# Half tiles of the output projection between the last three value products of attention, and its inputs by groups in a fixed order

## The chip, the cores and the metric

The kernel runs on one core of a Trainium2 chip. The core has five engines with a queue each: TensorE (PE, matrix products), VectorE (DVE), ScalarE (ACT), GpSimd (POOL), and SyncE (SP), which here issues the transfers (DMAs). The time of a run is the device time in microseconds. The kernel before takes 3853.54 us, the median of 3 runs (3845.11 to 3853.94). The profile is of one further execution, which took 3845.32 us, with a span of 3843.2 us from its first to its last instruction.

## The reference

The input x has shape 2 x 48 x 48 x 768 in fp32: two images (batches), 2304 tokens each, 768 channels. Two layers follow each other, each added to its input:

```python
x = x + _L0_conv_ref(_gn(x), qkv_w, qkv_b, proj_w, proj_b, rel_pos_h, rel_pos_w)
x = x + _L1_conv_ref(_gn(x), w1, b1, w2, b2)
```

`_gn` is a group norm over 32 groups of 24 channels. Layer 0 is attention with 12 heads of 64 channels over all 2304 tokens, with a relative position bias by row and by column, and an output projection:

```python
attn = einsum('bqc,bkc->bqk', q * scale, k) + rel_h[..., :, None] + rel_w[..., None, :]
out = softmax(attn) @ v          # heads put side by side
return out @ proj_w + proj_b
```

Layer 1 takes a two-dimensional Fourier transform of the image, applies two small complex matrix layers with a GELU between them to 8 blocks of 96 channels, shrinks small values to zero, and transforms back.

## The kernel before

Each batch goes through attention, the projection and the spectral layer, one after the other.

**Attention** works on two heads (a pair, six of them) and 128 queries at a time. This is a unit; there are 108 of them, numbered n = 0 to 107, and the loop of `attention` runs to n = 110, since a unit's work is spread over three iterations. In iteration n:

- `scores(n)`: TensorE multiplies queries by keys (ps_s), and VectorE adds the bias tile s in place and keeps the maximum.
- `numerators(n)`: ScalarE takes the exponential of s.
- `weigh(n - 2)`: TensorE multiplies the turned numerators pT of the unit two before by the values v (ps_o). This is the value product. The code weighs unit n - 2 at iteration n, so units 105, 106 and 107 have their value products at n = 107, 108 and 109, the last two without scores beside them.
- `squares` and `exchange` of unit n - 1, second half, and of unit n, first half: VectorE turns 32 x 32 squares, and each half goes into pT by 6 transfers from SyncE and 2 copies on ScalarE. The first half of unit n waits until the value product of unit n - 2 has read the buffer that it takes, since there are two pT buffers.
- `finish(n - 2)`: ScalarE copies ps_o out, and after every third unit SyncE stores a piece of the attention output to oT in memory.
- `new_unit(n + 1)` (line 340): GpSimd makes the next bias tile s from rhw. There are three s buffers, so it waits for the exchange of unit n - 2.
- `inverses`: after each half of a pair, the inverses of the softmax sums are turned (ps_i), copied and stored to inv_d.
- At n = 102 to 108 the loop calls `late()`, which makes one step of the projection's preparation.

The names pe, dve, act and sync in `attention` are `InOrder` objects: every instruction that they issue is pinned behind whatever was written before it for the same engine. Line 67 is the helper's, so most of attention's instructions are recorded on it. Instructions called on `nc` directly are not pinned in front, and a scheduler with a cost model places them before the build is finished; a pinned instruction written later still stays behind them.

**Projection.** `Projection` takes over the memory of the normed input, once no unit reads it any more. It holds the weights w (two transfers, lines 585 and 586), a bias row for all partitions, pb, and two buffers for groups of attention output. `tokens(g)` loads group g (384 tokens, three tiles of 128) from oT (line 631) and the inverses from inv_d (line 633, two transfers into one buffer), and GpSimd scales the group (line 637). The seven steps before are: weights, weights, nothing, `tokens(0)`, nothing, the bias row, `values_bias`. The last works for batch 0 only: the value bias goes through the weights (24 matmul instructions, ps_pb, line 612), VectorE adds both halves to pb (line 619), and the row is kept in memory (pb_d, line 621) for batch 1, which loads it with line 600.

`project_out` then loads the rows of x (x2, six groups of 4 x 96 tokens, line 653), and GpSimd adds pb to each of the four (line 655). All six groups' loads are written ahead of the loop. For each tile t of 18 and each half of the channels (a half tile, 384 columns), TensorE accumulates acc from six pairs of instructions (line 691) in a PSUM bank, and VectorE adds it to the rows (line 700), by pieces of 32 to 96 rows. The pool ps_b has 7 PSUM banks. When two more rows of x2 are complete, `over_w` makes the first Fourier transform of them (ps_y, line 671, 8 instructions), ScalarE copies it (line 678), and SyncE stores it to y_d (line 679). When a row is complete, `tile_stats` computes its group sums: VectorE reduces (line 724) and scales (line 725), GpSimd subtracts (line 727), ScalarE squares (line 730), VectorE reduces (line 731). None of the instructions of `project_out` is pinned.

**Spectral** takes the rest; its transfers of weights (line 844) may be placed among the projection's.

Of the kernel before, what the change touches and what calls it, by code (L numbers as in the profile page):

```python
# [9 lines left out]
F32 = mybir.dt.float32  # L10
# [6 lines left out]
P = 128  # L17
# [140 lines left out]


def attention(tc, k, x_b, a, oT, inv_d, late, span, ps_b, ps_o):  # L160

# [10 lines left out]
    with ExitStack() as ctx:  # L172
# [319 lines left out]
        for n in range(len(order) + 3):  # L492
            un = older = None
            if n < len(order):
                un = ahead
                pr, g, x = order[n]
                if g == 4 and x == 0 and pr + 1 < NP:
                    weights[0] = load_w(0, pr + 1)
                scores(un)
                recent.append(un)  # L500
            write = read = None
            if un is not None:
                numerators(un)
                ready, staged = staged, None
                if x == 2:
                    if n + 4 < len(order):
                        key = order[n + 4][:2]
                        staged = (key, queries(*key))
                    if g == 2 and pr + 1 < NP:
                        weights[2] = load_w(2, pr + 1)  # L510
                    if g == 5 and pr + 2 < NP:
                        weights[1] = load_w(1, pr + 2)
                elif n < 2:
                    for i in range(3):
                        values(0, 3 * n + i)
                    if n:
                        weights[1] = load_w(1, 1)
                elif pr + 1 < NP:
                    i = 2 * g + x
                    for j in range(0 if n == 3 else i, i + 1):  # L520
                        (keys if j < 6 else values)(pr + 1, j % 6)
                if ready is not None:
                    key, qT = ready
                    rhw, write, read = relative(key[1], qT)
                    groups[key] = (qT, rhw)
            if turn is not None:
                turn()
                turn = None
            if n > 1 and recent:
                older = recent.pop(0)  # L530
                weigh(older)
            evict(by_act)
            if last is not None:
                squares(last, 1)
                exchange(last, 1)
            if write is not None:
                write()
            if un is not None:
                squares(un, 0)
# [30 lines left out]
class Projection:  # L570


    def __init__(self, tc, k, a, oT, inv_d, span, ps_b, dram):
        self.nc = nc = tc.nc
        self.k, self.a, self.ps_b, self.dram = k, a, ps_b, dram
        self.oT_v = oT.rearrange("(cc p) s -> p cc s", p=P)
        self.inv_d = inv_d
        self.whole = span.tile([P, NCC * S], F32, tag="span", name="proj")
        self.w = self.whole[:, : NCC * C].rearrange("p (cc f) -> p cc f", f=C)
        self.pb = self.whole[:, NCC * C : (NCC + 1) * C]  # L580
        self.o = {}
        w_v = a["proj_w"].rearrange("(cc p) f -> p cc f", p=P)
        half = NCC // 2
        self.steps = [
            lambda: nc.sync.dma_start(out=self.w[:, :half], in_=w_v[:, :half]),
            lambda: nc.sync.dma_start(out=self.w[:, half:], in_=w_v[:, half:]),
            lambda: None,
            lambda: self.tokens(0),
            lambda: None,
            self.bias,  # L590
            self.values_bias,
        ]

    def step(self):
        self.steps.pop(0)()

    def bias(self):

        src = self.a["proj_b"] if self.k.pb_d is None else self.k.pb_d
        self.nc.sync.dma_start(out=self.pb, in_=src.partition_broadcast(P))  # L600

    def values_bias(self):


        nc, k = self.nc, self.k
        if k.pb_d is not None:
            return
        for hf in range(2):
            cols = slice(hf * UQ, (hf + 1) * UQ)
            ps = self.ps_b.tile([P, 512], F32, tag="b", name="ps_pb")  # L610
            for cc in range(NCC):
                nc.tensor.matmul(
                    ps[:, :UQ],
                    lhsT=k.bv[:, cc : cc + 1].to_broadcast([P, P]),
                    rhs=self.w[:, cc, cols],
                    start=(cc == 0),
                    stop=(cc == NCC - 1),
                )
            nc.vector.tensor_tensor(self.pb[:, cols], ps[:, :UQ], self.pb[:, cols], ALU.add)
        k.pb_d = self.dram.tile([C], F32, tag="pb_d", name="pb_d")  # L620
        nc.sync.dma_start(out=k.pb_d, in_=self.pb[0, :])

    def tokens(self, g):

        nc = self.nc
# [5 lines left out]
        nc.sync.dma_start(out=o_sb, in_=self.oT_v[:, :, g * UQ : (g + 1) * UQ])  # L631
        for h in range(2):
            nc.sync.dma_start(
                out=inv[h * HD : (h + 1) * HD],
                in_=self.inv_d[:, g // 3, h, g % 3, :].partition_broadcast(HD),
            )
        nc.gpsimd.tensor_tensor(o_sb, o_sb, inv, ALU.mult)  # L637
        self.o[g] = o_sb


def project_out(tc, k, x_b, pr, pools, y_d, x2, stats, constants):

# [18 lines left out]
    dev = small.tile([R, HW // 2, NG], F32, tag="dev", name="dev")  # L661
# [1 line left out]
    def over_w(g):  # L663

        y1 = work.tile([YP, 2, C], F32, tag="y1", name="y1")
        part = x2[2 * g // XP]
        t0 = 2 * g % XP
        for s in range(C // SC):
            ch = slice(s * SC, (s + 1) * SC)
            ps = bank("ps_y")  # L670
            nc.tensor.matmul(
                ps[:YP, : 2 * SC],
                lhsT=k.fw,
                rhs=part[:, t0 : t0 + 2, ch],
                start=True,
                stop=True,
            )
            nc.scalar.copy(y1[:, :, ch], ps[:YP, : 2 * SC].rearrange("p (t c) -> p t c", c=SC))
        nc.sync.dma_start(out=y_d[:, 2 * g : 2 * g + 2, :], in_=y1)

    done = turned = 0
    for t in range(NT):
        if t % 3 == 0:
            if t // 3 not in pr.o:
                pr.tokens(t // 3)
            o_sb = pr.o[t // 3]
        for hf in range(2):
            cols = slice(hf * UQ, (hf + 1) * UQ)
            acc = bank("acc")
            for cc in range(NCC):  # L690
                nc.tensor.matmul(  # L691
                    acc[:, :UQ],
                    lhsT=o_sb[:, cc, (t % 3) * P : (t % 3 + 1) * P],
                    rhs=pr.w[:, cc, cols],
                    start=(cc == 0),
                    stop=(cc == NCC - 1),
                )
            for p, hp, q, n in shifts(t):
                dst = row(hp)[q : q + n, cols]
                nc.vector.tensor_tensor(dst, acc[p : p + n, :UQ], dst, ALU.add)  # L700
# [62 lines left out]
class Spectral:  # L763
# [50 lines left out]
    def bank(self, name):  # L814
        return self.ps_b.tile([P, 512], F32, tag="b", name=name)
# [211 lines left out]
def block_kernel(tc, a, out):  # L1027
    nc = tc.nc
    B = a["x"].shape[0]
    with ExitStack() as ctx:  # L1030
# [20 lines left out]
        for b in range(B):  # L1051
# [6 lines left out]
            def late():  # L1058
                if not ready:
                    ready.append(Projection(tc, k, a, oT, inv_d, span, ps_b, dram))  # L1060
                ready[0].step()

            attention(tc, k, a["x"][b], a, oT, inv_d, late, span, ps_b, ps_o)
            with ExitStack() as ctx2:
# [115 lines left out]
```

## Time and profile before

| what | value |
|---|---|
| median of 3 runs | 3853.54 us (3845.11 to 3853.94) |
| the profiled execution | 3845.32 us, span 3843.2 us |
| busy: PE / PEld / DVE / ACT / POOL | 95% / 68% / 77% / 65% / 54% |
| chain that ended last, by engine | PE 81%, DMA 6%, DVE 5%, POOL 4%, SP's queue 2% |
| batch 0: end of the last value product, end of the projection's last ps_y | 1472.97 us, 1661.35 us |
| batch 1: the same | 3388.3 us, 3580.5 us |
| DMA share, 1385 to 1405 / 1425 to 1445 / 1495 to 1505 us | 0.98 / 1.02 / 1.04 |

The timeline of an engine has, on each line, the start and the duration in us, the engine, the line of the code, the operation, output<-inputs, the memory shapes and the number of instructions merged; in brackets stands the idle time of the engine ahead of it and who ended it. PE's instructions in fp32 go in pairs, so a half tile is 12 of them. A table by stretches has for each stretch its length, the engine's busy time, the granted clock of TensorE as a share of full speed, the mean busy share of the 16 DMA engines and GB/s.

### The profile page before, as it was taken

What the parts mean: (1) busy time and instruction counts of PE and PEld (TensorE: products, weight loads), DVE (VectorE), ACT (ScalarE), POOL (GpSimd) and SP (SyncE); (2) the same over time, 40 slices, a digit from 0 to 9 for tenths busy, and PEclk for the clock granted to TensorE, in tenths of its full rate; (3) what the DMA queues carried; (4) which work ended last, traced back from release to release, by engine and by line L of the source; (5) the groups of instructions that cost most, each with busy time, mean ns of one, the idle gap of its engine ahead of it and who ended that gap; (6) DMA issues with size and microseconds to landing.
All of it is one profiled execution on the core that took longest, in us unless ns stands there. A gap on an engine that the chain in (4) does not pass through costs nothing.

```text
span 3843.2 us, 83225 instructions
## 1 busy us (share of the span) xinstructions
PE 3661.7 (95%) x31464; PEld 2599.0 (68%) x31464; DVE 2950.0 (77%) x6642; ACT 2502.4 (65%) x3549; POOL 2063.9 (54%) x646
## 2 busy tenths in 40 slices
PE   8999999999999988989989999999999999779898
PEld 6677776767777655567566777777677776555675
DVE  4788888888889885654457988889888899846544
ACT  3688888888888882222137888888888888812221
POOL 2466666666666666321125666666666666663111
PEclk9999999999999999999989999999999999889899
DMA  3677777777777888434526777777777777884344
GB/s 100 143 174 169 173 171 167 175 165 178 167 171 171 172 195 199 126 90 119 165 83 138 172 174 169 174 167 174 168 174 168 173 170 168 202 195 114 90 119 133
DMA packets 496092, 606.92 MB, mean 158 GB/s; under 512 B 180109, under 2 KB 310797, under 8 KB 495694
## 3 DMA queue, kind: packets, MB, share of 16 engines
q1 hardware_dynamic: 495694, 601.61, 67.2%
q8 instruction: 250, 4.10, 0.5%
q14 instruction: 148, 1.21, 0.1%
HBM read 131.53 MB, written 87.67 MB: 57 GB/s over the span
## 4 chain that ended last, share of the span: by engine, by line
PE 81%; DMA 6%; DVE 5%; POOL 4%; SPq 2%; issue 1%; ACT 1%; POOLq 0%; DVEq 0%; ACTq 0%
PE ps_o L67 20%; PE ps_s L67 19%; PE ps_proj L67 14%; PE ps_v L67 8%; PE acc L691 5%; DVE s L67 4%; PE ps L926 4%; POOL s L340 3%; DMA pT<-s 2%; SPq L67 2%; PE ps_z L874 2%; PE ps_u L957 2%; PE ps_x L981 2%; PE ps L899 2%; PE ps L903 2%; PE ps_r L67 1%
## 5 line engine op out<-in xcount | busy, mean ns | idle before, releaser
L340 POOL TENSOR_TENSOR s<-rhw 128x2304 f32<-128x2304 f32 x432 | 1744.8, 4060 | 1152.1 <-DMA pT<-s 552.7
L67 DVE CUSTOM_DVE_ANT_0 s<-ps_s,s 128x512 f32<-128x512 f32 (+1 forms) x2160 | 1223.5, 633 | 372.9 <-issue 247.9
L67 ACT ACTIVATE s<-s,nm 128x1152 f32<-128x1152 f32 x864 | 1074.7, 1245 | 448.3 <-DVE nm L67 409.4
L67 DVE STREAM_TRANSPOSE s<-s 128x1152 f32<-128x1152 f32 x864 | 1111.8, 1344 | 5.5 <-ACT s L67 5.5
L67 ACT COPY pT<-s 32x1152 f32<-32x1152 f32 x864 | 993.3, 1150 | 24.5 <-PE ps_o L67 9.1
L67 PE MATMUL ps_o<-pT,v 128*64 128x128 f32 x15552 | 923.8, 279 | 70.8 <-DMA pT<-s 49.7
L67 PEld LDWEIGHTS ps_o<-pT,v 128*64 128x64 f32 x15552 | 872.0, 140 | 134.1 <-issue 66.1
L67 PE MATMUL ps_s<-kT,qT 64*128 64x512 f32 (+1 forms) x4320 | 918.2, 559 | 13.5 <-DVE mx L67 10.1
L67 PEld LDWEIGHTS ps_s<-kT,qT 64*128 64x128 f32 x4320 | 431.5, 187 | 449.7 <-issue 334.2
L67 PE MATMUL ps_proj<-xnT,w 128*128 128x384 f32 (+1 forms) x2016 | 600.2, 452 | 3.7 <-ACT gn_rstd L148 3.7
L67 PEld LDWEIGHTS ps_proj<-xnT,w 128*128 128x128 f32 x2016 | 362.4, 192 | 211.9 <-DVE mx L67 41.0
L691 PE MATMUL acc<-proj 128*128 128x384 f32 x864 | 292.0, 498 | 25.5 <-POOL proj L637 14.9
L67 PEld LDWEIGHTS ps_v<-w,xnT 128*128 128x128 f32 x2592 | 295.5, 193 | 21.5 <-DVE mx L67 21.5
L67 PE MATMUL ps_v<-w,xnT 128*128 128x128 f32 x2592 | 307.7, 279 | 0.0
L943 POOL TENSOR_TENSOR spectrum<-spectrum 128x480 f32<-128x480 f32 x80 | 96.3, 1204 | 325.8 <-DVE spectrum L942 322.1
L691 PEld LDWEIGHTS acc<-proj 128*128 128x128 f32 x864 | 168.4, 196 | 145.6 <-issue 20.4
L730 ACT ACTIVATE st_xc<-st_xc 96x768 f32<-96x768 f32 x48 | 40.5, 843 | 234.6 <-POOL st_xc L727 234.6
L67 DVE DVE_READ_ACCUMULATOR2_ANT mx<- 128x1 f32 x2160 | 179.4, 83 | 0.0
L700 DVE TENSOR_TENSOR x<-acc,x 32x384 f32<-32x384 f32 (+2 forms) x216 | 119.6, 553 | 77.6 <-PE acc L691 73.5
L67 ACT ACTIVATION_READ_ACCUMULATOR s<-s,nm 128x1 f32 x864 | 161.2, 187 | 0.0
L907 ACT ACTIVATE spectrum<-ps,b 96x400 f32<-96x400 f32 x96 | 56.5, 589 | 140.1 <-PE ps L903 140.1
L727 POOL TENSOR_TENSOR st_xc<-x,local 96x768 f32<-96x768 f32 x48 | 70.9, 1481 | 142.9 <-DVE local L725 120.9
(96 smaller groups left out, 2217.8 us busy)
## 6 DMA issues: line engine op xcount, KB each, us to landing
pT<-s SPq DMA_DIRECT2D x2592, 144.0 KB
t<-rel SPq DMA_DIRECT2D x144, 189.0 KB
rhw<-t SPq DMA_DIRECT2D x144, 144.0 KB
y_d<-y SPq DMA_DIRECT2D x24, 672.0 KB
y<-y_d SPq DMA_DIRECT2D x40, 360.0 KB
u_d<-spectrum SPq DMA_DIRECT2D x40, 360.0 KB
u<-u_d SPq DMA_DIRECT2D x48, 300.0 KB
xt<-in_x SPq DMA_DIRECT2D x12, 1152.0 KB
```

The lines of the kernel that those rows point to most:

```text
L67: return lambda *args, **kw: self.tc.keep_in_program_order(op(*args, **kw))
L340: nc.gpsimd.tensor_tensor(s[:, h, :].rearrange("p (y x) -> p y x", x=HW), rhw[:, x, h, :HW][:, :, None].to_broadcast([P, HW, HW]), rhw[:, ...
L691: nc.tensor.matmul(acc[:, :UQ], lhsT=o_sb[:, cc, (t % 3) * P : (t % 3 + 1) * P], rhs=pr.w[:, cc, cols], start=(cc == 0), stop=(cc == NCC - 1),
L700: nc.vector.tensor_tensor(dst, acc[p : p + n, :UQ], dst, ALU.add)
L727: nc.gpsimd.tensor_tensor(xc, x3, local[:, :, None].to_broadcast([xt.shape[0], NG, GC]), ALU.subtract)
L874: nc.tensor.matmul(ps[:BS, w * 96 : (w + 1) * 96], lhsT=self.y2[s, j][:, w, i * BS : (i + 1) * BS], rhs=k.fh, start=True, stop=True,)
L899: nc.tensor.matmul(ps[:BS, :400], lhsT=w1[:, wa, i, :], rhs=zf[:, 0, fs], start=True, stop=False,)
L903: nc.tensor.matmul(ps[:BS, :400], lhsT=w1[:, wb, i, :], rhs=zf[:, 1, fs], start=False, stop=True,)
L926: nc.tensor.matmul(ps[64 * r : 64 * r + 64, w * BS : (w + 1) * BS], lhsT=self.o1[:, ri, f0 : f0 + 64], rhs=w2[:, (0, 2, 1, 0)[2 * r + ri], ...
L943: nc.gpsimd.tensor_tensor(val, val, clip, ALU.subtract)
L957: nc.tensor.matmul(ps[: 2 * HW, :480], lhsT=k.ih, rhs=d2[:, c0 : c0 + 480], start=True, stop=True)
L981: nc.tensor.matmul(ps[: 2 * HW, : 2 * SC], lhsT=k.iw, rhs=self.u2[s, i][:, t : t + 2, :], start=True, stop=True,)
```

## The change

1. *Filling.* `Projection` gets a list `waiting`: for batch 0 the two halves of `values_bias`, then the half tiles of tiles 0 to 2; for batch 1 the half tiles alone. The attention loop takes from it ahead of the last three value products: one at n = 107, two at n = 108, two at n = 109. Batch 0 so makes both bias halves and three half tiles there, batch 1 five half tiles. A new function `product(t, hf)` makes a half tile's accumulation and keeps its bank until `project_out` adds it to the rows.
2. *Steps.* The seven steps become: weights, weights, `tokens(0)`, the bias row, nothing, nothing, `tokens(1)`. So group 0 is loaded at n = 104 instead of 105, the bias row at n = 105 instead of 107, and group 1 at n = 108, where it came with `project_out` before.
3. *Groups one ahead.* `project_out` loads two groups of rows ahead of the loop (the constants between them). At tiles 3, 6, 9 and 12 it loads the next group of attention output and then the next group of rows.
4. *Fixed order.* The matmuls of the half tiles, the bias and `over_w`, the loads of groups and rows, the stores to y_d, and the scaling and row additions on GpSimd go through `InOrder` objects.

```diff
+            if n >= len(order) - 1 and recent:
+                late(1 if n < len(order) else 2)
             if n > 1 and recent:
                 older = recent.pop(0)
                 weigh(older)
...
+        self.pe, self.sync, self.pool = (
+            InOrder(tc, e) for e in (nc.tensor, nc.sync, nc.gpsimd)
+        )
         self.steps = [
             lambda: nc.sync.dma_start(out=self.w[:, :half], in_=w_v[:, :half]),
             lambda: nc.sync.dma_start(out=self.w[:, half:], in_=w_v[:, half:]),
+            lambda: self.tokens(0),
+            self.bias,
             lambda: None,
-            lambda: self.tokens(0),
             lambda: None,
-            self.bias,
-            self.values_bias,
+            lambda: self.tokens(1),
         ]
+        self.accs, self.waiting = {}, []
+        if k.pb_d is None:
+            self.waiting += [lambda hf=hf: self.values_bias(hf) for hf in range(2)]
+        for t in range(3):
+            self.waiting += [lambda t=t, hf=hf: self.product(t, hf) for hf in range(2)]
...
+    def fill(self, n):
+
+        for _ in range(n):
+            self.waiting.pop(0)()
...
+    def product(self, t, hf):
+
+        if (t, hf) not in self.accs:
+            o_sb = self.o[t // 3]
+            acc = self.ps_b.tile([P, 512], F32, tag="b", name="acc")
             for cc in range(NCC):
-                nc.tensor.matmul(
+                self.pe.matmul(
+                    acc[:, :UQ],
+                    lhsT=o_sb[:, cc, (t % 3) * P : (t % 3 + 1) * P],
+                    rhs=self.w[:, cc, hf * UQ : (hf + 1) * UQ],
                     start=(cc == 0),
                     stop=(cc == NCC - 1),
                 )
+            self.accs[t, hf] = acc
+        return self.accs[t, hf]
...
-    for i, part in enumerate(x2):
-        nc.sync.dma_start(out=part, in_=x_v[:, i * XP : (i + 1) * XP, :])
+
+    def rows(i):
+
+        part = x2[i]
+        pr.sync.dma_start(out=part, in_=x_v[:, i * XP : (i + 1) * XP, :])
         for j in range(XP):
-            nc.gpsimd.tensor_tensor(part[:, j, :], part[:, j, :], pr.pb[:R], ALU.add)
-        if i == 0:
-            constants()
-            pr.tokens(1)
+            pr.pool.tensor_tensor(part[:, j, :], part[:, j, :], pr.pb[:R], ALU.add)
+
+    rows(0)
+    constants()
+    rows(1)
...
     for t in range(NT):
-        if t % 3 == 0:
-            if t // 3 not in pr.o:
-                pr.tokens(t // 3)
-            o_sb = pr.o[t // 3]
+        if t % 3 == 0 and 0 < t < NT - 3:
+            pr.tokens(t // 3 + 1)
+            rows(t // 3 + 1)
         for hf in range(2):
             cols = slice(hf * UQ, (hf + 1) * UQ)
-            acc = bank("acc")
...
+            acc = pr.product(t, hf)
```

More of the change, by code (lines that the diff above doesn't have):

```diff
@@ L600, in bias, with values_bias @@
         self.nc.sync.dma_start(out=self.pb, in_=src.partition_broadcast(P))
-    def values_bias(self):
+    def values_bias(self, hf):
         nc, k = self.nc, self.k
[L606 to L610, printed above, removed]
+        cols = slice(hf * UQ, (hf + 1) * UQ)
+        ps = self.ps_b.tile([P, 512], F32, tag="b", name="ps_pb")
+        for cc in range(NCC):
+            self.pe.matmul(
+                ps[:, :UQ],
+                lhsT=k.bv[:, cc : cc + 1].to_broadcast([P, P]),
+                rhs=self.w[:, cc, cols],
+                start=(cc == 0),
+                stop=(cc == NCC - 1),
+            )
+        nc.vector.tensor_tensor(self.pb[:, cols], ps[:, :UQ], self.pb[:, cols], ALU.add)
+        if hf:
+            k.pb_d = self.dram.tile([C], F32, tag="pb_d", name="pb_d")
+            nc.sync.dma_start(out=k.pb_d, in_=self.pb[0, :])
+    def product(self, t, hf):
+        if (t, hf) not in self.accs:
+            o_sb = self.o[t // 3]
+            acc = self.ps_b.tile([P, 512], F32, tag="b", name="acc")
             for cc in range(NCC):
[L612 to L615, printed above, removed]
+                self.pe.matmul(
+                    acc[:, :UQ],
+                    lhsT=o_sb[:, cc, (t % 3) * P : (t % 3 + 1) * P],
+                    rhs=self.w[:, cc, hf * UQ : (hf + 1) * UQ],
                     start=(cc == 0),
@@ L618, in values_bias @@
                 )
-            nc.vector.tensor_tensor(self.pb[:, cols], ps[:, :UQ], self.pb[:, cols], ALU.add)
-        k.pb_d = self.dram.tile([C], F32, tag="pb_d", name="pb_d")
-        nc.sync.dma_start(out=k.pb_d, in_=self.pb[0, :])
+            self.accs[t, hf] = acc
+        return self.accs[t, hf]
     def tokens(self, g):
-        nc = self.nc
         at = [(NCC + 1) * C + i * NCC * UQ for i in range(3)]
@@ L630, in tokens @@
         )
-        nc.sync.dma_start(out=o_sb, in_=self.oT_v[:, :, g * UQ : (g + 1) * UQ])
+        self.sync.dma_start(out=o_sb, in_=self.oT_v[:, :, g * UQ : (g + 1) * UQ])
         for h in range(2):
-            nc.sync.dma_start(
+            self.sync.dma_start(
                 out=inv[h * HD : (h + 1) * HD],
@@ L636, in tokens @@
             )
-        nc.gpsimd.tensor_tensor(o_sb, o_sb, inv, ALU.mult)
+        self.pool.tensor_tensor(o_sb, o_sb, inv, ALU.mult)
         self.o[g] = o_sb
@@ L670, in over_w @@
             ps = bank("ps_y")
-            nc.tensor.matmul(
+            pr.pe.matmul(
                 ps[:YP, : 2 * SC],
@@ L678, in over_w @@
             nc.scalar.copy(y1[:, :, ch], ps[:YP, : 2 * SC].rearrange("p (t c) -> p t c", c=SC))
-        nc.sync.dma_start(out=y_d[:, 2 * g : 2 * g + 2, :], in_=y1)
+        pr.sync.dma_start(out=y_d[:, 2 * g : 2 * g + 2, :], in_=y1)
     done = turned = 0
     for t in range(NT):
-        if t % 3 == 0:
-            if t // 3 not in pr.o:
-                pr.tokens(t // 3)
-            o_sb = pr.o[t // 3]
+        if t % 3 == 0 and 0 < t < NT - 3:
+            pr.tokens(t // 3 + 1)
+            rows(t // 3 + 1)
         for hf in range(2):
             cols = slice(hf * UQ, (hf + 1) * UQ)
-            acc = bank("acc")
[L690 to L697, printed above, removed]
+            acc = pr.product(t, hf)
             for p, hp, q, n in shifts(t):
@@ L1056, in block_kernel, with late @@
             ready = []
-            def late():
+            def late(fill=0):
                 if not ready:
                     ready.append(Projection(tc, k, a, oT, inv_d, span, ps_b, dram))
-                ready[0].step()
+                if fill:
+                    ready[0].fill(fill)
+                else:
+                    ready[0].step()
             attention(tc, k, a["x"][b], a, oT, inv_d, late, span, ps_b, ps_o)
```

## The prediction

> **What bounds the kernel now.** I read the page first, then the TensorE timeline around the end of attention in each batch, then the same stretch for GpSimd, SyncE and VectorE, and last the table by stretches. On the page TensorE is busy 95% of the span and holds 81% of the chain that ended last; what a change can win is TensorE's idle time and half-clock time. TensorE, end of batch 0's attention and start of its projection (start, us, operation, in brackets the idle time before it and who ended it):
>
> ```profile
> 1439.83 1.92 PE L67 MATMUL ps_s<-kT,qT 64*128 64x512 f32 x6 [0.60 <-DVE mx L67]
> 1441.68 8.01 PE L612 MATMUL ps_pb<-proj,bv 128*128 128x384 f32 x24
> 1450.15 4.15 PE L67 MATMUL ps_o<-pT,v 128*64 128x128 f32 x72 [0.47 <-ACT s L67]
> 1458.54 6.71 PE L67 MATMUL ps_o<-pT,v 128*64 128x128 f32 x72 [4.23 <-DMA pT<-s]
> 1468.82 4.15 PE L67 MATMUL ps_o<-pT,v 128*64 128x128 f32 x72 [3.57 <-DMA pT<-s]
> 1473.02 31.13 PE L691 MATMUL acc<-proj 128*128 128x384 f32 x96
> ...
> 1529.60 7.04 PE L691 MATMUL acc<-proj 128*128 128x384 f32 x12 [8.68 <-DVE x L700]
> 1541.57 10.06 PE L691 MATMUL acc<-proj 128*128 128x384 f32 x24 [4.93 <-POOL proj L637]
> ```
>
> The last scores end at 1441.75, the three last value products (ps_o, units 105 to 107) stand apart, and the projection itself stops twice. Batch 1 has the same shape without ps_pb:
>
> ```profile
> 3362.53 7.03 PE L67 MATMUL ps_o<-pT,v 128*64 128x128 f32 x72 [6.34 <-DMA pT<-s]
> 3372.24 5.62 PE L67 MATMUL ps_o<-pT,v 128*64 128x128 f32 x72 [2.68 <-DMA pT<-s]
> 3382.84 5.45 PE L67 MATMUL ps_o<-pT,v 128*64 128x128 f32 x72 [4.98 <-DMA pT<-s]
> ...
> 3459.00 10.49 PE L691 MATMUL acc<-proj 128*128 128x384 f32 x24 [9.97 <-POOL proj L637]
> ```
>
> GpSimd: the bias tile of unit 107 (L340) and the scaling of group 0 (L637), of each batch:
>
> ```profile
> 1430.43 8.08 POOL L340 TENSOR_TENSOR s<-rhw 128x2304 f32<-128x2304 f32 x2 [1.66 <-DMA pT<-s]
> 1447.40 5.13 POOL L637 TENSOR_TENSOR proj<-proj 128x2304 f32<-128x2304 f32 x1 [8.89 <-DMA proj<-inv_d]
> ...
> 3344.72 8.07 POOL L340 TENSOR_TENSOR s<-rhw 128x2304 f32<-128x2304 f32 x2 [2.02 <-ACT res L67]
> 3358.26 5.09 POOL L637 TENSOR_TENSOR proj<-proj 128x2304 f32<-128x2304 f32 x1 [5.46 <-DMA proj<-inv_d]
> ```
>
> SyncE's queue, where group 0's loads stand behind the exchange of unit 105's first half:
>
> ```profile
> 1408.09 23.53 SPq L67 DMA_DIRECT2D pT<-s  x24
> 1431.67 0.59 SPq L631 DMA_DIRECT2D proj<-oT  x1
> 1432.30 1.49 SPq L633 DMA_DIRECT2D proj<-inv_d  x2
> ```
>
> VectorE, two L725 during runs of GpSimd row additions: one got in after 1.26 us, one only after 10.22:
>
> ```profile
> 1502.48 1.26 DVE L725 TENSOR_SCALAR local<-local 96x32 f32<-96x32 f32 x1
> 1514.04 10.22 DVE L725 TENSOR_SCALAR local<-local 96x32 f32<-96x32 f32 x1
> ```
>
> The stretches from the end of the last value product to the projection's last matmul, both batches (length, PE busy, clock, DMA share, GB/s):
>
> ```profile
> 1472.97:1661.35 188.38, 174.76 (x526) 0.95 0.54 138
> 3388.30:3580.50 192.20, 176.90 (x529) 0.96 0.52 134
> ```
>
> Pure work there: 36 half tiles of 3.87 us (31.13 is eight) = 139.3, and 12 transforms of 2.58 = 31.0, together 170.3. So 18.1 and 21.9 us are idle or at half clock.
>
> **What the Trainium skill says.** "SBUF — State Buffer", Who interferes with whom: a VectorE tensor_scalar in a 2-port mode and a GpSimd instruction take one shared port pair as an exclusive lock, and the second blocks. The trace agrees (10.22 us against 0.18 undisturbed). "TensorE: Matmul & The Clock Gate", What's actually happening: about 3.4 us of idling halves the clock until as long a busy window. It agrees: 12 matmuls took 7.04 us after 8.68 idle. Same page, Architectural detail: VectorE, ScalarE and GpSimd are strict FIFO, so a waiting instruction holds all behind it. GpSimd's lines agree.
>
> **The change, part by part.**
>
> *Filling.* 3 half tiles (batch 0, with both bias halves, which stood there before) and 5 (batch 1) leave the stretch after the last value product: 3 x 3.87 = 11.6 and 5 x 3.87 = 19.4 us. Left after it: 33 half tiles + transforms = 127.7 + 31.0 = 158.7, and 31: 120.0 + 31.0 = 151.0.
>
> *Group 0's loads one iteration earlier* (n = 104, not 105). Three transfers issue in 2.0 us in SyncE's idle stretch from 1419.9, ahead of the second-half exchange of unit 104 (1423.86). By the semaphore records transfers land nearly in issue order: the exchange's pieces every 0.75 us, and group 0's three took 12.7 us (1434.5 to 1447.2) in batch 0, 9.5 in batch 1. Before, they delayed unit 105's second half only, and no bias tile came after it. Now they delay unit 104's, which frees the buffer that unit 107's bias tile needs. Batch 0: queue free at 1424.1, group 0 landed at 1436.8, exchange at 1439.3. GpSimd scales group 0 first (5.1 us, to 1441.9), then L340 runs 1441.9 to 1450.0 instead of 1430.4 to 1438.5. Scores end at 1452.6, against 1441.75. Batch 1: landed 3347.5, scaled to 3352.6, L340 to 3360.7 (before 3352.8), scores end 3363.3, against 3356.2.
>
> *TensorE's fixed order from there*, gapless. Batch 0: 2 x 4.0 (bias) + 3 x 3.87 + 3 x 4.15 = 32.1, so the last value product ends at 1484.7, **11.7 later** than 1472.97. Batch 1: 5 x 3.87 + 12.45 = 31.8, 3395.1, **6.8 later** than 3388.3. Does the data come? Batch 0's exchanges: VectorE's bias addition (0.55, now ahead of the transposes of L67) ends at 1457.3, the transposes at 1459.8 and 1462.4, SyncE issues 6 pieces in 3.85; unit 107's second half waits for the second bias addition (1465.3), lands near 1474.5, needed at 1480.5. Covered by 6 us; were that gone, it would be lost one for one. The waits added here: on VectorE the two bias additions wait for TensorE, and behind the second stand unit 107's last transposes (before at 1449.96), then their exchange, then the last value product. On TensorE each value product now waits behind half tiles, and its copy to SBUF and the inverses behind it: that is the 11.7 and 6.8. The 0.64 us bias issue moves two iterations up, into a lull: nothing.
>
> *Row loads after the inverses.* Before, row group 0 was issued at 1465.94 and landed at 1473.51, 7.6 later. Now it stands in SyncE's order behind the inverses' three stores: the last value product, 0.8 for the copy, 2.4 for the stores, 7.6: 10.8 us after that product. Two row additions (2 x 1.77) and VectorE (0.6) free the first PSUM bank at 15.0. There are 7. Batch 0 holds 3 and fills 4 more until 15.6: no wait. Batch 1 holds 5, fills two by 7.8 and waits 7.2. Then the first transform (after the fourth tile, in fixed order) needs tiles 0 and 1 added: row statistics and six more additions, at 21.5. TensorE gets there at 19.5 and 18.9: waits 2.0 and 2.6. L725 is the unknown: it may slip in at the next instruction's end (counted) or be held to the end of eight row additions, 25.2, 7 us more. Nothing excludes either; of six L725 in such runs four slipped in. I take half, 3.5 a batch, and 1.5 for the clock at half speed.
>
> *Groups one ahead.* From tile 3 on, a group's TensorE time is 6 x 3.87 + 2 x 2.58 = 28.4. Loads issued at its start land after 11.5, are scaled by 16.6, rows added by 23.7 (four of 1.77): hidden with 11.8 and 4.7 to spare. GpSimd needs 5.1 + 7.1 + 4 x 1.48 = 18 of 28.4. The stops of 8.68, 4.93 and 9.97 go; they are in the 188.4 and 192.2. If that cover goes, each hand-over costs what it is late. Stores of y_d in fixed order wait for work already done: nothing.
>
> **Sum.** Batch 0: 188.4 - 11.7 - 158.7 - 2.0 - 5.0 = 11.0. Batch 1: 192.2 - 6.8 - 151.0 - 9.8 - 5.0 = 19.6. Together 30.6, say 30, off the profiled execution's 3845.3 (span 3843.2): 3815. Of the three runs shown one lies with it and two 8 us above, which makes the median 3853.5; I take the middle, **3819**.
>
> **Rivals.**
> *A, bias tile not delayed*: the small exchange pieces pass the big loads, L340 starts on time. For: transfers overlap in part. Against: unit 105's pieces issued at 1436.6 landed at 1447.9. It gives back up to 11.7 and 6.8: 49 off, about 3801.
> *B, scaling queued ahead of unit 106's bias tile too*: GpSimd then waits for group 0's landing with two bias tiles behind it. L340 of 106 starts at 1441.9 instead of 1420.7, unit 107's scores end 8 to 9 us later still, twice 9. With L725 held in both batches (7): about 5 off, 3844. For: the scaling is pinned in front. Against: unit 106's tile is not pinned and is ready first.
> *C, slower*: every group hand-over late. GpSimd scales and adds strictly in order, so a load that lands late holds row additions and statistics, and fixed-order TensorE stops. Eight hand-overs (four a batch); 30 / 8 = 3.8 us each decides, that is loads landing near 27 us instead of 11.5. At 6 each: 48 - 30, 18 slower, 3863 to 3872. For: at the start the queue is full (a row group waited 30 us in it). Against: that was five row groups at once; now one.
>
> **How the numbers follow.** Likeliest 0.55, A 0.15, B 0.17, C 0.13. Likeliest alone: 3805 to 3835 (L725 both ways, either run level). Range: 3792 (A with both L725 free) to 3852 (B with the upper level). Three runs spread by 0.23%, so 0.3% (11.6 us) is about what can be told from no change: all of the likeliest and A, a little of B are faster, 0.73; most of B same, 0.14; C slower, 0.13.
>
> **What would show it.** Right: no ps_o with idle before it at the end of attention; L340 of unit 107 some 8 to 11 us later against its predecessors; L725 and a bank wait near 8 to 30 us after the last ps_o; no idle at L637 afterwards. Wrong: unit 107's tile on time (A), a POOL wait on proj<-inv_d before unit 106's tile (B), TensorE waiting on POOL or DVE at every third tile (C), or value products that still wait for pT.

## The result, and the profile after

The changed kernel takes **3835.99 us** (median, 3832.68 to 3840.88), beside 3852.39 us of the kernel before in the same comparison (3845.11 to 3855.07): a ratio of **0.9964**, 95% interval 0.9952 to 0.9976. It is 16.4 us faster; 3819 and about 30 us (34.5 between the prediction's 3819 and the median of before that it used, 3853.5) had been forecast. Two later comparisons gave 0.9965 and 0.9971. The direction was right, and about half of the gain is there.

First the page of the profiled execution of the changed kernel: its span, and TensorE's row (busy time, share of the span, instructions).

```profile
span 3834.6 us, 83183 instructions
PE 3656.9 (95%) x31464; PEld 2586.8 (67%) x31464; DVE 2940.0 (77%) x6642; ACT 2496.3 (65%) x3549; POOL 2063.2 (54%) x646
```

The span is 8.6 us shorter than before's 3843.2. The forecast for this pair was 30.6, so 22 us have to be found. (The profiled execution of before took 3845.32 us, well under its kernel's median of 3852.39, which is why this pair shows less than the medians.)

TensorE's timeline at the end of batch 0's attention, to be held against the first view of the prediction:

```profile
1451.15 4.14 PE L67 MATMUL ps_pb<-proj,bv 128*128 128x384 f32 x12
1455.22 4.15 PE L67 MATMUL ps_o<-pT,v 128*64 128x128 f32 x72
1459.30 4.14 PE L67 MATMUL ps_pb<-proj,bv 128*128 128x384 f32 x12
...
1471.32 8.01 PE L67 MATMUL acc<-proj 128*128 128x384 f32 x24
1479.26 4.15 PE L67 MATMUL ps_o<-pT,v 128*64 128x128 f32 x72
```

No value product waits any more, and the last one ends at 1483.4. GpSimd's timeline shows why the scores end 9.5 us later: the bias tile of unit 107 (L341 now) comes after the scaling of group 0, which had waited for its load.

```profile
1436.03 5.07 POOL L67 TENSOR_TENSOR proj<-proj 128x2304 f32<-128x2304 f32 x1 [8.02 <-DMA proj<-inv_d]
1441.06 8.07 POOL L341 TENSOR_TENSOR s<-rhw 128x2304 f32<-128x2304 f32 x2
```

Both went as worked out (1441.9 for the bias tile, 1484.7 for the last value product). Now the table by stretches, from the end of the last value product to the last transform, both batches (length, then busy time and instructions of PE, PEld, DVE, ACT and POOL, granted clock, DMA share, GB/s):

```profile
1483.41:1660.28 176.87, 165.22 (x493) 91.73 (x493) 116.84 (x179) 37.20 (x71) 102.17 (x57) 0.98 0.57 145
3393.45:3568.68 175.23, 160.53 (x469) 89.48 (x469) 115.56 (x176) 37.74 (x71) 99.69 (x56) 0.95 0.58 146
```

Of 158.7 and 151.0 us of pure TensorE work they are 18.2 and 24.2 us too long; 7.0 and 14.8 had been forecast. (In the kernel before, batch 0's last transform ends at 1662.61 us, not at 1661.35 as the table of before and the prediction have it. Its stretch is 189.6 us, and the prediction's sum for batch 0 is 1.3 us too small.) The start is as foreseen. This is batch 1's bank wait on TensorE's timeline, 7.12 us against a forecast of 7.2:

```profile
3408.52 5.85 PE L67 MATMUL acc<-proj 128*128 128x384 f32 x12 [7.12 <-DVE x L726]
```

The surplus lies further on, in the steady groups of three tiles. Three timelines of one group of batch 0 show it, GpSimd first (L753 is the subtraction of the row statistics, the x4 line the four row additions):

```profile
1581.10 5.07 POOL L67 TENSOR_TENSOR proj<-proj 128x2304 f32<-128x2304 f32 x1
1586.13 7.09 POOL L67 TENSOR_TENSOR x<-x,proj 96x768 f32<-96x768 f32 x4
1593.17 1.49 POOL L753 TENSOR_TENSOR st_xc<-x,local 96x768 f32<-96x768 f32 x1
```

VectorE, which made the mean of that row at 1587 (L751), then stands at the second reduction of the same statistics (L757):

```profile
1587.34 0.64 DVE L751 TENSOR_SCALAR local<-local 96x32 f32<-96x32 f32 x1
1595.57 0.95 DVE L757 TENSOR_REDUCE dev<-st_xc 96x32 f32<-96x768 f32 x1 [7.59 <-ACT st_xc L756]
1596.53 4.56 DVE L726 TENSOR_TENSOR x<-acc,x 32x384 f32<-32x384 f32 x8
```

In the kernel before, the reduction at the same place of a group (L731 there) waited 2.53:

```profile
1595.69 0.95 DVE L731 TENSOR_REDUCE dev<-st_xc 96x32 f32<-96x768 f32 x1 [2.53 <-ACT st_xc L730]
```

In the changed kernel TensorE then runs out of PSUM banks, because the eight additions that start at 1596.53 (L726), which empty them, are queued behind that reduction:

```profile
1581.05 15.66 PE L67 MATMUL acc<-proj 128*128 128x384 f32 x48
...
1598.93 0.87 PE L67 MATMUL ps_y<-x,fw 96*112 96x384 f32 x2 [0.29 <-DVE x L726]
1601.23 8.29 PE L67 MATMUL acc<-proj 128*128 128x384 f32 x24 [1.43 <-DVE x L726]
```

So: GpSimd's scaling and four row additions, 12.2 us in one piece, stand ahead of the subtraction. VectorE needs the square of what the subtraction leaves, and waits 7.59 us for it. The same point of VectorE's loop comes round at 1577.29 and 1608.19, every 30.9 us, while TensorE's share of a group is 28.4. The Trainium skill says why such a wait spreads ("TensorE: Matmul & The Clock Gate", Architectural detail: VectorE's and ScalarE's queues are strictly first in, first out). The trace agrees: VectorE fell idle at 1588.0, the half tile that the first four additions need was done by about 1585 (an estimate, 1581.05 and 3.87), and none of them went ahead of the reduction.

The kernel before had no such block at this place. Its last row addition ended at 1532.95 us (batch 1: 3448.28), and TensorE did the groups behind that at 28.4 us each without a stop (1579.86 to 1608.24). The change takes the old stops ahead of those groups away and puts the additions of four of the six row groups among the steady groups. That is a reading of traces; the runs below test it.

### The profile page after: what moved, and what is told of

Same layout as the page of the kernel before. It is cut to its first block, busy times and chain, and to the rows that moved or that the text cites. A ratio compares the mean times of both kernels' runs of the same rounds, so it can differ in the third digit from the quotient of the medians.

```text
span 3834.6 us, 83183 instructions
## 1 busy us (share of the span) xinstructions
PE 3656.9 (95%) x31464; PEld 2586.8 (67%) x31464; DVE 2940.0 (77%) x6642; ACT 2496.3 (65%) x3549; POOL 2063.2 (54%) x646
## 5 line engine op out<-in xcount | busy, mean ns | idle before, releaser
L341 POOL TENSOR_TENSOR s<-rhw 128x2304 f32<-128x2304 f32 x432 | 1744.7, 4060 | 1146.8 <-DMA pT<-s 548.7
L67 PE MATMUL ps_s<-kT,qT 64*128 64x512 f32 (+1 forms) x4320 | 916.1, 558 | 15.3 <-DVE mx L67 11.7
L726 DVE TENSOR_TENSOR x<-acc,x 32x384 f32<-32x384 f32 (+2 forms) x216 | 119.2, 553 | 69.2 <-POOL x L67 64.4
L753 POOL TENSOR_TENSOR st_xc<-x,local 96x768 f32<-96x768 f32 x48 | 71.1, 1482 | 136.0 <-DVE local L751 135.5
```

The source lines that it names most:

```text
L67: return lambda *args, **kw: self.tc.keep_in_program_order(op(*args, **kw))
L341: nc.gpsimd.tensor_tensor(s[:, h, :].rearrange("p (y x) -> p y x", x=HW), rhw[:, x, h, :HW][:, :, None].to_broadcast([P, HW, HW]), rhw[:, ...
L753: nc.gpsimd.tensor_tensor(xc, x3, local[:, :, None].to_broadcast([xt.shape[0], NG, GC]), ALU.subtract)
```

## The experiments

**Two theories.** Theory 1: in the changed kernel VectorE's queue bounds the projection, through the statistics that wait behind GpSimd's block. Theory 2, the prediction's view: TensorE bounds it, a group costs 28.4, and the lost time is elsewhere (a late hand-over, the end of attention); then half tiles done ahead count one for one. Every kernel computes the whole result. Each was timed beside the kernel before on the same chip; the changed kernel and the one with spread additions ran again as levels. In the table "105 to VP" is the time from the start of unit 105's bias tile on GpSimd to the end of the last value product, "projection" from there to the last transform's end, batch 0 / batch 1, from each kernel's profile.

| kernel | median, us | before beside it | ratio (95%) | 105 to VP | projection |
|---|---|---|---|---|---|
| before | | | 1 | 65.2 / 67.1 | 189.6 / 192.2 |
| the change, first run | 3835.99 | 3852.39 | 0.9964 (0.9952 to 0.9976) | 76.6 / 75.9 | 176.9 / 175.2 |
| the change, beside 1, 3, 4 | 3835.74 | 3848.93 | 0.9965 (0.9953 to 0.9978) | 74.7 / 76.0 | 176.3 / 177.2 |
| the change, beside 2 | 3837.10 | 3847.27 | 0.9971 (0.9962 to 0.9980) | 75.3 / 73.8 | 177.0 / 176.5 |
| 1 additions spread | 3810.04 | 3848.93 | 0.9898 (0.9884 to 0.9911) | 74.4 / 75.0 | 163.7 / 164.7 |
| 1 again, beside 5, 7 | 3813.19 | 3851.59 | 0.9902 (0.9888 to 0.9915) | 74.4 / 75.9 | 163.4 / 163.3 |
| 1 again, beside 6, 8 | 3809.61 | 3848.82 | 0.9903 (0.9888 to 0.9917) | 73.7 / 75.1 | 163.6 / 164.6 |
| 2 half of them spread | 3809.74 | 3847.27 | 0.9906 (0.9893 to 0.9920) | 74.2 / 74.2 | 163.5 / 164.7 |
| 3 loads back at 105 | 3839.33 | 3848.93 | 0.9970 (0.9959 to 0.9982) | 74.0 / 76.4 | 175.8 / 177.0 |
| 4 no half tiles | 3841.78 | 3848.93 | 0.9978 (0.9968 to 0.9988) | 69.9 / 70.1 | 184.9 / 185.0 |
| 5 = 1, no half tiles | 3816.52 | 3851.59 | 0.9910 (0.9896 to 0.9923) | 69.8 / 70.3 | 170.5 / 171.0 |
| 6 = 5, loads at 105 | 3807.74 | 3848.82 | 0.9894 (0.9879 to 0.9909) | 70.0 / 64.2 | 170.5 / 170.5 |
| 7 = 1, two rows early | 3806.29 | 3851.59 | 0.9881 (0.9867 to 0.9894) | 74.7 / 73.6 | 160.4 / 160.5 |
| 8 = 6, three half tiles | 3809.38 | 3848.82 | 0.9901 (0.9884 to 0.9917) | 71.4 / 64.7 | 169.0 / 168.7 |

The level of the changed kernel had been expected like this, and lay there, with batch 1's projection 2 us longer:

> The changed kernel again, as the level for the runs beside it. Both theories: 0.995 to 0.998 of the kernel before, that is 8 to 19 us below it; from the last value product to the last transform 176.9 us in batch 0 and 175.2 in batch 1, as in its first profile.

**1. The row additions spread.** Loads and scaling stay where the change put them; the new lines stand behind the statistics of tile t.

```diff
-            rows(t // 3 + 1)
+            load_rows(t // 3 + 1)
...
+        if t % 3 and 3 < t < NT - 3:
+            add_bias(t // 3 + 1, range(2 * (t % 3) - 2, 2 * (t % 3)))
```

> The additions of a row group, four in a row behind its scaling until now, are spread: two after the statistics of the group's second tile, two after those of its third (from tile 4 on). Loads and scaling stay. Theory 1 (VectorE's queue bounds the projection, because its second reduction of the statistics waits behind GpSimd's scaling and four row additions): that wait falls from 7.6 us to about 2.5, a group of three tiles from 30.9 us to TensorE's 28.4, TensorE stops waiting for VectorE from the third tile on; 10 to 20 us faster than the changed kernel, 0.991 to 0.994 of the kernel before. Theory 2 (the projection is bound by TensorE, the lost time is elsewhere): no change, within 3 us of the changed kernel.

Measured: 25.7 us faster than the changed kernel beside it, more than the 10 to 20 expected, and 0.990 of the kernel before in three comparisons. The same reduction on VectorE (L764 here), and TensorE in a later group:

```profile
1579.39 0.95 DVE L764 TENSOR_REDUCE dev<-st_xc 96x32 f32<-96x768 f32 x1 [2.54 <-ACT st_xc L763]
```

```profile
1590.13 2.75 PE L67 MATMUL ps_y<-x,fw 96*112 96x384 f32 x8
1592.71 7.91 PE L67 MATMUL acc<-proj 128*128 128x384 f32 x24
1600.45 2.75 PE L67 MATMUL ps_y<-x,fw 96*112 96x384 f32 x8
1603.03 15.64 PE L67 MATMUL acc<-proj 128*128 128x384 f32 x48
1618.51 2.75 PE L67 MATMUL ps_y<-x,fw 96*112 96x384 f32 x8
```

The wait is back at 2.54, no bracket is left on TensorE in this part, and the transform comes round after 28.4 us (1590.13 to 1618.51). The projections are 12.6 and 12.5 us shorter than those of the changed kernel beside it, 25.1 together, close to the 25.7 between the medians. Theory 2 expected no change and falls for the steady part.

**2. Only half of them spread**: two additions stay behind the scaling, two come after the statistics of the group's third tile. If VectorE is a bound that stands over TensorE's by 2.5 us a group, half of the cure must bring all of the gain; if each addition in the block, or each meeting of GpSimd and VectorE, had its own cost, half of it. The edit is to run 1's code.

```diff
             load_rows(t // 3 + 1)
+            add_bias(t // 3 + 1, range(2))
...
-        if t % 3 and 3 < t < NT - 3:
+        if t % 3 == 2 and 3 < t < NT - 3:
-            add_bias(t // 3 + 1, range(2 * (t % 3) - 2, 2 * (t % 3)))
+            add_bias(t // 3 + 1, range(2, XP))
```

> Only half of the additions are moved: of a row group's four, two stay behind the scaling and two come after the statistics of the group's third tile. Theory 1 (a bound: VectorE's loop of 30.9 us stands over TensorE's 28.4, and every us of GpSimd work taken out of the block comes off VectorE's loop): the block shrinks by 3.55 us, the loop to 27.3, TensorE is the bound again, and nearly the whole gain of the full spread is there: 20 to 26 us faster than the changed kernel. Rival (a cost for each addition in the block, or a conflict of GpSimd and VectorE while they run): half of the gain, 10 to 14 us.

Measured: 27.4 us faster than the changed kernel beside it, all of the gain. The reduction on VectorE:

```profile
1582.39 0.95 DVE L765 TENSOR_REDUCE dev<-st_xc 96x32 f32<-96x768 f32 x1 [4.08 <-ACT st_xc L764]
```

The wait is 4.08, which is 7.59 less 3.51, for two additions of 1.78 fewer in the block. GpSimd's subtraction ahead of the two moved additions starts at 1564.26, 1591.65 and 1619.02, every 27.4 us where 27.3 had been expected for the loop. That is under 28.4: VectorE catches up with TensorE, whose transform comes round every 28.4 and does not wait. So a bound was crossed, and it was the loop of VectorE and GpSimd.

**3. Group 0's loads back at 105**, the half tiles staying between the value products. (The bias row's load moves with them, from 105 to 106.)

```diff
             lambda: nc.sync.dma_start(out=self.w[:, half:], in_=w_v[:, half:]),
+            lambda: None,
             lambda: self.tokens(0),
             self.bias,
             lambda: None,
-            lambda: None,
             lambda: self.tokens(1),
```

> Group 0's loads and scaling go back by one iteration of attention, to the place that they had before; the half tiles still stand between the value products. If the loads' transfers are what delays unit 107's bias tile (my step), that tile starts about 10 us earlier in batch 0 and 7 in batch 1, and the scores end by as much earlier; but group 0 is scaled later, so the half tiles wait: the last value product ends only about 5 us earlier in batch 0 and 1 in batch 1, together 5 to 8 us faster than the changed kernel. Rival (the transfers are not the cause): scores end as in the changed kernel, no gain, and the half tiles wait for the scaling, 5 to 15 us slower.

Measured: 3.6 us slower than the changed kernel, with intervals that overlap: no gain. GpSimd's timeline in batch 0 and TensorE's in batch 1:

```profile
1434.70 8.08 POOL L341 TENSOR_TENSOR s<-rhw 128x2304 f32<-128x2304 f32 x2 [1.85 <-DMA pT<-s]
1451.61 5.06 POOL L67 TENSOR_TENSOR proj<-proj 128x2304 f32<-128x2304 f32 x1 [8.83 <-DMA proj<-inv_d]
```

```profile
3364.42 6.65 PE L67 MATMUL acc<-proj 128*128 128x384 f32 x12 [6.60 <-POOL proj L67]
```

Unit 107's bias tile starts 22.9 us after unit 105's, where the three profiles of the changed kernel have 32.3 to 34.2 (batch 1: 23.2, and 31.4 to 33.6). So the loads were indeed what delayed it, by some 8 to 11 us. But the half tiles, fixed ahead of the value products, now wait for the scaling, 6.60 us here, and the last value product ends hardly sooner: 74.0 and 76.4 us after the start of unit 105's tile, against 74.7 to 76.6 and 73.8 to 76.0. With half tiles in that place the delay is paid in one coin or the other. My expected 5 to 8 us were a miss.

**4. No half tiles in the filling**, all else as changed.

```diff
-        for t in range(3):
-            self.waiting += [lambda t=t, hf=hf: self.product(t, hf) for hf in range(2)]
...
         for _ in range(n):
-            self.waiting.pop(0)()
+            if self.waiting:
+                self.waiting.pop(0)()
```

> No half tiles between the last three value products (batch 0 keeps its two bias halves there); they are computed in the projection itself. Theory 1 (VectorE's queue bounds the projection, which ends some 165 us after the first row group landed, however many half tiles TensorE has done by then): the last value product ends 5 us earlier in batch 0 and 0 to 8 in batch 1, the row group lands by as much earlier, and the projection ends by as much earlier: 3 to 13 us faster than the changed kernel. Theory 2 (bound by TensorE): eight half tiles of 3.87 us are missing from the filling, 31 less 5 to 13: 18 to 26 us slower than the changed kernel, slower than the kernel before.

Measured: 6.0 us slower than the changed kernel, with intervals that just overlap. Neither expectation holds. Against the changed kernel beside it the last value products end 4.9 and 5.8 us sooner, and the projections are 8.6 and 7.9 longer: 5.8 us net. I had let VectorE's chain set the end from the first row group on, whatever TensorE has done by then. Up to the fifth row that is so: in batch 0 its second reduction starts 44.2 us after the last value product here and 44.1 in the changed kernel's first profile. Then they part. Here tile 3's scaling and four additions stand in one piece on GpSimd, from 1522.16 to 1534.29 us, between the subtractions of the fifth and the sixth row, and VectorE waits 7.93 us for the sixth:

```profile
1536.96 0.95 DVE L756 TENSOR_REDUCE dev<-st_xc 96x32 f32<-96x768 f32 x1 [7.93 <-ACT st_xc L755]
```

In the changed kernel the fifth subtraction stands between that scaling and those additions, and the sixth reduction waits 2.35. So the kernel without half tiles enters the 30.9 us loop one group sooner, and its ninth reduction comes 7.7 us later after the last value product. The statistics are not pinned; why the build placed them otherwise was not tried.

So eight half tiles, 31 us of work, are worth about 6 here.

**5. Spread additions without half tiles** (edits 1 and 4 together) asks what the filling is worth once TensorE is the bound.

> Spread row additions, and no half tiles between the value products (batch 0 keeps its bias halves). Theory 1: TensorE is now the bound in the steady part, but at the start half tiles only move ahead into a wait for banks and rows (5.0 and 13.7 us above the pure work with the half tiles, about 1 without); projection 171 to 172 us in each batch against 163.7 and 164.7, value products end 5 and 6 us earlier: 2 to 5 us slower than the kernel with spread additions. Theory 2 (once TensorE is the bound, every half tile that leaves the filling comes back in full): 31 less 11, 18 to 22 us slower.

Measured: 3.3 us slower than with them, with intervals that overlap; theory 1's 2 to 5, not 18 to 22. The half tiles move out of the projection (7.1 and 7.7 us shorter) into the end of attention (4.6 and 5.6 us longer); the rest of the 31 turns into waits for rows and banks.

**6. Also group 0's loads at 105**: edits 1, 3 and 4, so that of the change the fixed order, with the bias halves in it, and the groups one ahead are left (with them the earlier bias row and group 1).

> Spread row additions, no half tiles, and group 0's loads and scaling back in their old place, one iteration of attention later (batch 0 keeps its bias halves in fixed order). Against the kernel with the half tiles and the earlier loads (spread additions in both). Theory 1 (what the half tiles and the earlier loads win in the projection they have cost before it): the last value products end as in the kernel before, some 9 to 11 us earlier per batch; the projection takes 171 to 172 us instead of 164: 3 to 8 us faster. Theory 2 (the half tiles pay, TensorE being the bound): 10 us slower or more.

Measured: 1.9 us faster than edit 1 beside it, within the uncertainty: the same, where 3 to 8 had been expected. Its table by stretches, in the columns shown above:

```profile
1477.82:1648.36 170.54, 170.53 (x530) 98.85 (x529) 112.74 (x179) 40.01 (x71) 102.44 (x57) 1.00 0.61 153
3374.73:3545.26 170.53, 170.53 (x530) 98.86 (x529) 112.73 (x179) 39.81 (x71) 102.38 (x57) 1.00 0.60 152
```

TensorE is busy for the whole of both projections, at full clock, in 170.5 us, the prediction's pure work of 170.3. All the idle time that before had there is gone without a single half tile moved.

**7. Two row tiles early** (with edit 1): the first two of 24 are loaded into an unused end of the weights' buffer, in SyncE's order just ahead of group 1's loads, and VectorE adds from there.

```diff
-            lambda: self.tokens(1),
+            lambda: (self.first_rows(), self.tokens(1)),
...
-                nc.vector.tensor_tensor(dst, acc[p : p + n, :UQ], dst, ALU.add)
+                src = pr.x01[q : q + n, hp, cols] if hp < 2 else dst
+                nc.vector.tensor_tensor(dst, acc[p : p + n, :UQ], src, ALU.add)
```

> Spread row additions, and the first two of the 24 row tiles come into an unused part of the weights' buffer, loaded with the third group of transfers at the end of attention (ahead of group 1) instead of behind the inverses' stores; VectorE adds from there into the row group. Theory 1 (the start-up cost is the row group's late landing, 10.8 us after the last value product): the bank wait of batch 1 (7.2 us, and 1.5 of half clock behind it) goes, and of the 5.0 and 13.7 us above the pure work 2 to 4 stay in each batch: 8 to 12 us faster than the kernel with spread additions. Rival (the wait only moves to rows 2 and 3, which still land as late): under 3 us.

Measured: 6.9 us faster than edit 1 beside it, just short of the 8 to 12 expected. The bank wait of batch 1 is gone, but another has come:

```profile
3389.72 11.05 PE L67 MATMUL acc<-proj 128*128 128x384 f32 x24 [6.00 <-POOL proj L67]
```

GpSimd now does the two early additions and two subtractions of statistics ahead of group 1's scaling, and TensorE waits 6.00 us for that; the 24 matmuls behind it take 11.05 instead of 7.9, at half clock in part. (The Trainium skill, "TensorE: Matmul & The Clock Gate", What's actually happening: an idle stretch of about 3.4 us lowers the clock. The trace agrees.) This is the fastest kernel by its ratio, though its interval meets that of 6 and, barely, that of edit 1.

**8. Half tiles only where TensorE would stand idle** (on 6): one in batch 0, two in batch 1.

```diff
+        if k.pb_d is None:
+            self.waiting = [pb[0], pb[1], none, acc[0], none]
+        else:
+            self.waiting = [none, acc[0], none, acc[1], none]
```

> As the run before, but one half tile in batch 0 (ahead of the last value product) and two in batch 1 (ahead of the last two), where TensorE stands idle anyway. The value products then end no more than 2 us later a batch, and TensorE still comes to the first transform no sooner than the rows (27 and 23 us after the last value product against 21.5). Theory 1: nearly every one of the three half tiles counts, 3.87 each: 7 to 12 us faster than without half tiles, the fastest kernel. Rival (a half tile in a gap delays the product behind it, or the rows come later than TensorE): within 3 us.

Measured: 1.6 us slower than 6, the same within the uncertainty; the rival was right. The value products pay only 1.4 and 0.5 us, but the projections become only 1.5 and 1.8 us shorter, not 3.9 and 7.7: TensorE now reaches the first transforms before VectorE has emptied the banks and waits there, 1.78 us in batch 0 and 1.63 in batch 1.

## Why the prediction was half right

**Right, by its steps.**
- *Group 0's loads one iteration earlier* delay unit 107's bias tile: forecast 11.5 and 7.9 us, measured 11.5 and 10.0 against unit 105's (9.6 to 11.5 and 7.9 to 10.1 over the three profiles of the change). Run 3 took it back.
- *TensorE's fixed order, gapless*: the last value product 11.7 and 6.8 us later; measured 11.4 and 8.8. The three profiles have 9.5 to 11.4 and 6.7 to 8.9, so that a match within 0.3 us is in part luck.
- *Row loads after the inverses*: GpSimd's first row addition starts 10.9 us after the last value product in both batches (landing forecast at 10.8), no bank wait in batch 0 and 7.12 in batch 1.
- *Start of the projection*, with the 3.5 us for a held L725: 7.0 and 14.8 forecast; 5.0 and 13.7 in run 1, where nothing else is left. The hold itself never came in these rows (L758 in run 1 takes at most 1.74 us), so this half-counted term was a little too large.
- *The stops at the hand-over go*: yes; run 6 shows a projection without any.

**Wrong: the step "Groups one ahead", with the words "hidden with 11.8 and 4.7 to spare" and "GpSimd needs 5.1 + 7.1 + 4 x 1.48 = 18 of 28.4".** The loads came in time, as it said. But it compared GpSimd's sum of work with the time of a group and asked only whether TensorE would wait for the scaling. Scaling and additions are now fixed one behind the other ahead of the next statistics, and I did not name what is queued behind them on GpSimd (the subtraction) and who waits for that: VectorE, with its second reduction, and behind it the additions that free TensorE's banks. VectorE's slack of about 2.5 us a group was not in the sum either (28.4, against 30.9 less the 5.05 that the block adds to the wait). The prediction put this step at nothing. Measured, in batch 0, it costs some 2.5 us for a group and 4.5 more at the end; by the last row below (18.2 less 5.0, 24.2 less 13.7) it costs 13.2 us in batch 0 and 10.5 in batch 1:

| us (batch 0 / batch 1) | forecast | the change, first run | with additions spread |
|---|---|---|---|
| last value product later than before's | 11.7 / 6.8 | 11.4 / 8.8 | 9.2 / 7.9 |
| pure TensorE work after it | 158.7 / 151.0 | 158.7 / 151.0 | 158.7 / 151.0 |
| above the pure work | 7.0 / 14.8 | 18.2 / 24.2 | 5.0 / 13.7 |

The misses of the middle column are 11.2 + 9.4 = 20.6 in the last row (23.7 for the step, less 3.1 by which the start had been counted too high) and 1.7 in the first, 22.3 together. With the block taken apart the sum is 3810 to 3813 where 3815 to 3819 had been forecast.

**The rivals.** A did not come: unit 107's tile was delayed. B did not come: unit 106's tile ran ahead of the scaling. C had the mechanism, that strictly ordered GpSimd holds the statistics and TensorE stops, but tied it to late loads; it came with loads in time, and 22.3 / 8 = 2.8 us for each of its eight hand-overs, under the 3.8 from which it would have made the kernel slower.

**What was worth what.** The runs also say what the prediction's total had hidden. The half tiles, which give the change its name, are worth about 6 us as the change stands and 3 once VectorE is out of the way, both within or near the uncertainty, for 31 us of work moved; and with the earlier loads that they need, nothing that the timing can tell (run 6 against 1). The gain is in the groups one ahead and the fixed order, once the additions are spread: run 6, without half tiles, is 41 us faster than before. How it divides between those two was not tried.

## What to carry to other kernels

When work is moved to an engine's queue in a block, its sum against the period is not enough: take the instruction right behind the block, follow who waits for it and what is queued behind that wait, until an engine is met that has less slack than the block adds to its wait. A bound crossed by 2.5 us a group is undone by any cut that takes it below, so spread the block before looking for more work to hide. And work put into idle gaps counts only as far as the engine that uses its result can start sooner; here eight half tiles of 3.87 us were worth some 3 to 6 us.

## What the runs showed that I had not expected

- The wait followed GpSimd's block one for one until it reached its old value: 12.2 us of block gave 7.59 us at the reduction, 3.5 us less of it 4.08, and the spread additions 2.54, the value of the kernel before.
- VectorE's small L751, held for 10.22 us in the kernel before, was never held through a run of row additions in these profiles: beside them it took 0.63 to 1.46 us. What decides that was not tried and stays open.
- A TensorE stretch of 170.5 us without one idle microsecond ran at a granted clock of 1.00, with GpSimd and VectorE both busy for 60 to 66% of it.
